# Attention 2 of a two-layer model: context columns rotated on VectorE beside the query projections, and a schedule by half batches

## The chip, the cores and the metric

The kernel runs on one core of a Trainium2 chip. The metric is the device time of one execution in microseconds (us); the time before is the median of six runs. Engines are named as the profile names them: PE is TensorE (PEld its weight loads), DVE is VectorE, ACT is ScalarE, POOL is GpSimd, and SP is SyncE, whose queue issues most transfers.

## The reference, cut to what matters

Four blocks follow one another on x (8 batches of 100 tokens, 512 wide): attention 0, a mixture-of-experts block, attention 2, and a block with quantised weights. The change is in attention 2, which reads a context of 8 batches of 361 rows, 128 wide:

```python
def _L1_xattn_ref(hidden_q, kv_c, Wq, w_kc_q, w_kc_kv, W_qr, W_kr, Wo):
    q_hk = (hidden_q @ Wq.T).reshape(b, s, H, K)
    q_big = jnp.einsum('bshk,hkq->bshq', q_hk, w_kc_q)
    kv_rope = kv_c * cos[None] + _rotate_half(kv_c) * sin[None]
    q_r = jnp.einsum('bshq,hqr->bhsr', q_big, W_qr)
    k_r = jnp.einsum('bld,hdr->bhlr', kv_rope, W_kr)
    scores = jnp.einsum('bhsr,bhlr->bhsl', q_r, k_r)
    attn = jax.nn.softmax(scores, axis=-1)
    ctx_c = jnp.einsum('bhsl,bld->bhsd', attn, kv_rope)
    ctx_lat = jnp.einsum('bhsd,hkd->bshk', ctx_c, w_kc_kv)
    return ctx_lat.reshape(b, s, H * K) @ Wo.T
```

## The kernel before

Weights that follow one another are folded earlier in the kernel: `wqf` takes a normalised token to its query of every head, `wvo` takes the weighted context of all heads to the output. All of attention 2 is in float32. It has three stages.

**Query projections (loop around L1435).** The 800 tokens are seven row tiles, in three groups: tiles 0 and 1, tiles 2 and 3, tiles 4 to 6. For each group PE multiplies `wqf` with the transposed, normalised tokens, in chunks of 8 matmul records: four chunks of two head pairs each (`p0` = 0, 2, 4, 6) for the first two groups, eight chunks of one head pair (`p0` = 0 to 7) and 288 columns for the third. A chunk goes to one PSUM bank, and `evacuate` copies it out, on DVE and ACT in turn (L90, L92). While a group is projected, DVE and ACT normalise the tiles of the next one (`token_norms`: statistics L118 and L120, root L122 on ACT, reciprocal L129, scaling L132), and after chunk `p0 == 4` PE transposes them (`token_rows`, L1301).

**Rotation of the context, beside it.** For each batch SP loads 361 rows in three pieces (`context_in`, L1347; three buffers, so the load of batch b+3 waits until POOL is through with batch b). POOL rotates the rows with four `tensor_tensor` instructions (L1355, L1356, and L1358 twice) and stores them to DRAM, `ctx_rot` (L1359, L1360). From there SP loads them again in three forms: rows (`context_rows`, L1374, L1375), blocks of 32 rows for the values (`context_blocks`, L1384, L1389), and, from the rows, columns: `context_columns` has PE transpose three pieces (L1396), and ACT and DVE copy them out of PSUM to `kvT` (L1398, L1399).

**Scores and values.** `queries(b, h)` multiplies with W_kr for half of the heads of two batches at once (L1489, 16 records into the four banks of `four`), and DVE and ACT copy the result into the tile `qe` (L1495, L1499): for batch 0 in turn, for later batches on ACT alone. A batch has 12 score steps of 96 whole tokens (16 heads in 2 halves of 6 steps), and every even batch one more for the four leftover tokens of two batches. One score step is two PE records (L1524; L1519 for leftovers), a negated row maximum on DVE (L1529), the exponential with its sum on ACT (L1532), a reciprocal on DVE (L1538), the scaling of the probabilities on POOL (L1542; on ACT, L1540, for the first four), and a transpose by 32x32 squares on DVE (L1549). After a half batch's six steps `values(b, h)` multiplies them with the context: 96 records (L1558), copied out by ACT (L1564). Leftovers are transposed by PE (L1573), copied by ACT (L1576, L1577) and multiplied (L1585).

The order on PE, DVE and ACT is written out by hand (`manual_schedule`): step n issues scores(n), scaled(n-1) and turned_squares(n-3), and `due` puts everything else to a step. `values` come AHEAD = 7 steps behind the last score of their half. Also beside these steps, DVE quantises nine weight tiles of the next block (`quantise_steps`, L1598 to L1603), a third of its work per step. The order on SP and POOL is set by the scheduler from the order in the program and from what is free. Each engine carries out its own instructions in order. `tc.issue_after(d)` makes a load follow another on its queue.

## Time and profile before

| | us |
|---|---|
| Median of six runs | 633.34 |
| The six runs | 632.38, 638.66, 633.10, 642.20, 632.33, 633.58 |
| The profiled execution, its own time | 631.59 |
| Its span in the profile | 629.8 |
| Projections of the first group begin (L1435) | 274.5 |
| of the second group | 289.1 |
| of the third group | 304.45 |
| Projections end | 320.2 |
| First values begin (L1558) | 335.94 |
| Last records of attention 2 on PE end | 492.97 |
| From there to the end of the span | 136.8 |

All times inside the execution are from the start of its span. A table of windows lists, for a stretch of time, how long each engine was busy in it, the clock granted to PE (1.00 is full) and the share of the transfer engines' time. The chain of waits goes back from the last instruction to what released it, and so on; it is shown in order of time. A timeline lists one engine's instructions: start, duration, line and operation, out<-in with the shapes; in square brackets stands the idle time just before, with what ended it. An "x6" at the end of a line is a number of instructions put together.

### The profile page before, as it was taken

Reading aid. Unit: us, or ns where it says so; the run is one execution under the profiler, and the core shown is the slowest. Engines: PE = TensorE matmul, PEld = TensorE weight load, DVE = VectorE, ACT = ScalarE, POOL = GpSimd, SP = SyncE. Lnnn points to the kernel's source line nnn. Section 1 sums busy time; section 2 is a strip of 40 time slices with the busy share of each in tenths; the row PEclk is TensorE's granted clock in tenths of the full one; section 3 lists DMA queues with packets and bytes.
Section 4 is the critical chain, followed back from the end, with each engine's and each line's share of the span. In section 5 each row is a group of like instructions: output and inputs, shape, how many; then the busy total and the mean of one; then the engine's idle time right before and its main releaser. Section 6 shows DMA issues by size and latency. Waiting matters only on the chain.

```text
span 629.8 us, 12203 instructions
## 1 busy us (share of the span) xinstructions
PE 603.2 (96%) x4587; PEld 399.2 (63%) x4594; DVE 400.4 (64%) x1032; ACT 234.2 (37%) x545; POOL 241.6 (38%) x246
## 2 busy tenths in 40 slices
PE   8999999979999999999989999999989999999995
PEld 6767755557777776578856767776766644444442
DVE  4865688827777553254147676776776366766687
ACT  3653545651111111331246555556554121222130
POOL 1231331031333321118937676777786002222020
PEclk9999999999999999999999999999999999999999
DMA  8900094758999999663610322323111301101221
GB/s 291 317 26 18 7 324 146 232 167 227 341 303 272 232 294 332 133 197 90 161 34 2 99 73 40 85 74 97 51 37 28 136 11 31 24 17 24 52 38 69
DMA packets 90628, 80.79 MB, mean 128 GB/s; under 512 B 40939, under 2 KB 67263, under 8 KB 90439
## 3 DMA queue, kind: packets, MB, share of 16 engines
q1 hardware_dynamic: 86471, 70.61, 39.1%
q0 software_dynamic: 4096, 9.38, 7.2%
q8 instruction: 37, 0.61, 0.4%
q14 instruction: 24, 0.20, 0.1%
HBM read 62.27 MB, written 10.88 MB: 116 GB/s over the span
## 4 chain that ended last, share of the span: by engine, by line
PE 65%; DVE 8%; ACT 3%; issue 2%; POOL 1%; ACTq 0%; DVEq 0%
PE bank L389 13%; PE bank L1190 12%; PE four L1558 10%; PE bank L1435 7%; PE bank L1251 7%; PE bank L1524 6%; PE bank L1743 3%; PE bank L1291 2%; DVE sq L1549 2%; DVE nm L1529 2%; PE four L1489 1%; PE bank L1127 1%; ACT e L1532 1%; POOL hid L1760 1%; PE bank L395 1%
## 5 line engine op out<-in xcount | busy, mean ns | idle before, releaser
L1542 POOL TENSOR_SCALAR e<-e,rs 128x361 f32<-128x361 f32 x96 | 115.5, 1217 | 46.9 <-DVE rs L1538 45.1
L389 PE MATMUL bank<-wvo,ctxT 128*128 128x512 f32 x192 | 84.4, 594 | 0.0
L1529 DVE TENSOR_REDUCE nm<-bank 128x1 f32<-128x361 f32 x100 | 51.1, 512 | 36.9 <-PE bank L1524 29.1
L1524 PE MATMUL bank<-kvT,qe 128*128 128x361 f32 x192 | 70.2, 489 | 4.5 <-DVE qe L1495 2.5
L1190 PE MATMUL bank<-xgT,w 128*128 128x240 f32 (+1 forms) x384 | 74.1, 369 | 0.4 <-ACT xgT L1131 0.4
L1532 ACT ACTIVATE e<-bank,nm 128x361 f32<-128x361 f32 x100 | 56.7, 568 | 44.2 <-DVE rs L1538 44.2
L1190 PEld LDWEIGHTS bank<-xgT,w 128*128 128x128 f32 (+1 forms) x384 | 64.7, 181 | 11.5 <-issue 6.2
L1558 PEld LDWEIGHTS four<-sq,kv 32*128 32x128 f32 (+1 forms) x1536 | 62.3, 185 | 8.8 <-issue 4.9
L1558 PE MATMUL four<-sq,kv 32*128 32x192 f32 (+1 forms) x1536 | 66.9, 325 | 0.2
L389 PEld LDWEIGHTS bank<-wvo,ctxT 128*128 128x128 f32 x192 | 36.0, 190 | 42.6 <-issue 41.9
L1760 POOL TENSOR_TENSOR hid<-g,u 128x512 f32<-128x512 f32 (+1 forms) x17 | 20.4, 1216 | 110.1 <-ACT g L1751 108.6
L1549 DVE STREAM_TRANSPOSE sq<-e 128x384 f32<-128x384 f32 x96 | 53.5, 557 | 1.3 <-POOL e L1542 1.2
L1263 POOL DMA_INDIRECT x_acc<-y,place x16 | 25.1, 1571 | 75.3 <-ACT y L1262 45.2
L354 POOL TENSOR_TENSOR s<-s,rs 100x800 f32<-100x800 f32 x16 | 24.4, 1523 | 69.2 <-DVE rs L353 35.5
L1524 PEld LDWEIGHTS bank<-kvT,qe 128*128 128x128 f32 x192 | 32.4, 189 | 28.7 <-ACT e L1532 11.2
L1251 PE MATMUL bank<-w,hT 128*128 128x512 f32 (+3 forms) x96 | 42.8, 594 | 0.0
L1435 PE MATMUL bank<-xT,wqf 128*128 128x256 f32 (+1 forms) x128 | 29.8, 393 | 0.0
L1251 PEld LDWEIGHTS bank<-w,hT 128*128 128x128 f32 (+3 forms) x96 | 16.9, 183 | 20.0 <-issue 15.4
L1743 PE MATMUL bank<-w1q,xqT 128*128 128x512 bf16 (+1 forms) x140 | 29.1, 361 | 0.4 <-DMA xqT<-xq 0.2
L1435 PEld LDWEIGHTS bank<-xT,wqf 128*128 128x128 f32 x128 | 24.2, 190 | 4.9
L1748 DVE SCALAR_TENSOR_TENSOR g<-bank,sx,swb 128x512 f32<-128x512 f32 (+1 forms) x18 | 12.6, 702 | 19.0 <-PE bank L1743 18.4
L1201 ACT ACTIVATE silu<-bank 128x240 f32<-128x240 f32 x16 | 5.9, 370 | 50.1 <-PE bank L1190 46.7
(297 smaller groups left out, 965.2 us busy)
## 6 DMA issues: line engine op xcount, KB each, us to landing
w<-in_w SPq DMA_DIRECT2D x8, 1408.0 KB
gu<-in_wgu SPq DMA_DIRECT2D x22, 256.0 KB
wq_p<-in_wq SPq DMA_DIRECT2D x8, 512.0 KB
w<-in_w SPq DMA_DIRECT2D x16, 256.0 KB
wo<-in_wo SPq DMA_DIRECT2D x8, 512.0 KB
kq_p<-in_wkcq SPq DMA_DIRECT2D x16, 192.0 KB
kv<-ctx_rot SPq DMA_DIRECT2D x32, 96.0 KB
dn<-in_wdn SPq DMA_DIRECT2D x4, 704.0 KB
```

The costliest lines, as they stand in the source:

```text
L389: nc.tensor.matmul(po[:, :D], lhs[:, c, ds(t * P, r)], rhs[:, c, :], start=(c == 0), stop=(c == chunks - 1),)
L1190: nc.tensor.matmul(po, w12_e[:, c, cols], xgT[:, c, :], start=(c == c0), stop=(c == c1 - 1))
L1251: nc.tensor.matmul(py[i][:n], hT[:mr, m, ds(s0, n)], w3_e[:mr, m, :], start=(m == blocks[0]), stop=(m == blocks[2]),)
L1435: nc.tensor.matmul(pq[:, i, :], wqf[:, c, ts(p0 + i, P)], xT[:, c, :], start=(c == 0), stop=(c == KC - 1),)
L1524: nc.tensor.matmul(ps[:, :L], of_batch(b)[0][:, a, h, s].rearrange("p g q -> p (g q)"), kvTs[b], start=True, stop=True,)
L1529: nc.vector.tensor_reduce(nm, ps[:, :L], AX.X, ALU.max, negate=True)
L1532: nc.scalar.activation(e[:, :L], ps[:, :L], AF.Exp, bias=nm, accum_out=sm)
L1542: nc.gpsimd.tensor_scalar_mul(e[:, :L], e[:, :L], rs)
L1549: nc.vector.transpose(squares[b, h][:, a * (HT // 2) + s, :], e)
L1558: nc.tensor.matmul(pc[:, g, :cols].rearrange("p (t q) -> p t q", q=32), kv4s[b, j // NBH][ds(32 * g, n), j % NBH, :], eT[ds(32 * g, n), :, ...
L1743: nc.tensor.matmul(pw[:r, :n], xqT[:, c, :r], w1q[:, c, ds(off, n)], start=(c == 0), stop=(c == KC - 1),)
L1760: nc.gpsimd.tensor_tensor(hid[:r, ds(c0, n)], g[:r, :n], u[:r, :n], ALU.mult)
```

## The change

The reference's columns, rotated, are needed for the scores as `kvT` (128 x 361 a batch). The change takes them from a new path and orders the stage anew.

- **Columns.** For each batch SP loads the context as columns twice (`columns_in`: `same`, and `across` with its two halves exchanged; two buffers each), from the transposed input that attention 0 reads already. DVE multiplies both with tables of cosines and signed sines, adds them (`columns_turned`: three `tensor_tensor` of 128x361) and SP stores the result to DRAM, `ctx_rot_t`. `context_columns(b)` is now one load from there; the transposes on PE and the copies on ACT and DVE are gone. The rows are still rotated by POOL (`rotate(b)`), with the same instructions.
- **Where it is done.** `rotate` and `columns_turned` are called between the chunks of the first two groups of projections: behind p0 = 2, 4, 6 of the first (batches 0 to 2), behind p0 = 0, 2, 4 of the second (3 to 5) and twice behind its p0 = 6 (6, 7). In DVE's order they so stand among the copies of the chunks and the norms, and all of them ahead of the third group's copies. The tile `qe` of batches 0 and 1 comes from a pool, `first_pair`, that opens where the column tiles were.
- **Third group.** The PSUM banks of the scores are opened at its start; queries(0, 0) and queries(0, 1) follow its chunks p0 = 1 and 2, the scores 0 to 3 its chunks p0 = 4 to 7.
- **Half batches.** For half batch k there are six score steps, then the values of half batch k-1. Each half has at most one or two other jobs at fixed steps (`beside`): loads, queries (copied by DVE and ACT in turn, for all batches), the leftovers. The five DVE instructions of one quantised tile come in one piece behind the third step of nine halves. Leftover scores follow the values of odd halves of even batches. queries(2, 0) and queries(2, 1) move ahead of the first values.
- **Buffers.** `kv4` moves to a pool that opens after the projections, the quantised tile `gu_q` has one buffer instead of two, and the leftovers get a fifth tile of exponentials.

The diff, cut:

```diff
+    ctx_rot_t = tc.dram_tile([B, DC, L], F32, name="ctx_rot_t")
...
+    early, close_early = open_pool("attn1_early")
+    EP = 32 * ((L + 31) // 32)
+    es = [early.tile([P, EP], F32, tag=f"e{i}", name=f"e{i}") for i in range(4)]
...
+    contexts_in = [None]
+
     def context_in(b):
         kv = rot.tile([LP, LC, DC], F32, tag="kv", name=f"kv{b}")
         for c in range(LC):
-            nc.sync.dma_start(kv[:, c, :], ctx_n[b, ds(c * (LP - 1), LP), :])
+            d = nc.sync.dma_start(kv[:, c, :], ctx_n[b, ds(c * (LP - 1), LP), :])
+        contexts_in[0] = d.ins
         return kv
 
-    contexts = [context_in(b) for b in range(3)]
-    for b in range(B):
-        kv = contexts.pop(0)
+    def rotate(b, kv):
         kvr = rot.tile([LP, LC, DC], F32, tag="turned", name=f"turned{b}", bufs=2)
         low, high = slice(0, DC // 2), slice(DC // 2, DC)
         nc.gpsimd.tensor_tensor(kvr, kv, cos_sb, ALU.mult)
...
         nc.gpsimd.dma_start(
             ctx_rot[b, LP:].rearrange("(c p) d -> p c d", c=LC - 1), kvr[1:, 1:, :]
         )
-        if b + 3 < B:
-            contexts.append(context_in(b + 3))
+
+    contexts = [context_in(b) for b in range(3)]
...
-        kv4 = kvp.tile([P, NBH, DC], F32, tag="kv4", name=f"kv4_{b}_{h}", bufs=3)
+        kv4 = a1w.tile([P, NBH, DC], F32, tag="kv4", name=f"kv4_{b}_{h}", bufs=3)
...
-    def context_columns(b, kvr):
-        pt = bank()[:, : LC * LP].rearrange("p (c l) -> p c l", c=LC)
-        for c, (_, n) in enumerate(LCH):
-            nc.tensor.transpose(pt[:, c, :n], kvr[:n, c, :], ident[:n, :n])
+    colp, close_colp = open_pool("columns_in")
+    cos_col = colp.tile([P, L], F32, tag="cos_col", name="cos_col")
+    sin_col = colp.tile([P, L], F32, tag="sin_col", name="sin_col")
+    with tc.issue_after(contexts_in[0]):
+        nc.sync.dma_start(cos_col, rope_cos_t)
+        nc.sync.dma_start(sin_col, rope_sin_t)
+    columns_load = [None]
+
+    def columns_in(b):
+        same = colp.tile([P, L], F32, tag="same", name=f"same{b}", bufs=2)
+        nc.sync.dma_start(same, ctx_t[:, b, :])
+        across = colp.tile([P, L], F32, tag="across", name=f"across{b}", bufs=2)
+        nc.sync.dma_start(across[: DC // 2], ctx_t[DC // 2 :, b, :])
+        d = nc.sync.dma_start(across[DC // 2 :], ctx_t[: DC // 2, b, :])
+        columns_load[0] = d.ins
+        return b, same, across
+
+    def columns_turned(b, same, across):
+        nc.vector.tensor_tensor(across, across, sin_col, ALU.mult)
+        nc.vector.tensor_tensor(same, same, cos_col, ALU.mult)
+        nc.vector.tensor_tensor(same, same, across, ALU.add)
+        nc.sync.dma_start(ctx_rot_t[b], same)
+
+    def context_columns(b):
         kvT = kvp.tile([P, L], F32, tag="kvT", name=f"kvT{b}")
-        nc.scalar.copy(kvT[:, :LP], pt[:, 0, :])
-        nc.vector.tensor_copy(
-            kvT[:, LP:].rearrange("p (c l) -> p c l", c=LC - 1), pt[:, 1:, : LP - 1]
-        )
+        nc.sync.dma_start(kvT, ctx_rot_t[b])
...
-            qe = a1w.tile([P, 2 * NH1 * S], F32, tag="qe", name=f"qe{b}")
+            pool = a1w if b % 4 else first_pair
+            qe = pool.tile([P, 2 * NH1 * S], F32, tag="qe", name=f"qe{b}", bufs=1)
...
-        if n < 4:
+        if n < EARLY:
...
-        q = a1w.tile([P, D], BF16, tag="gu_q", name=f"gu_q{n}", bufs=2)
+        q = a1w.tile([P, D], BF16, tag="gu_q", name=f"gu_q{n}", bufs=1)
...
+    def next_columns(b):
+        kvTs[b] = context_columns(b)
+
+    def next_rows(b):
+        for k in range(2):
+            kvrs[b + k] = context_rows(b + k)
...
+    EARLY = 4
+
+    with tc.issue_after(contexts_in[0]):
+        columns = [columns_in(b) for b in range(2)]
+    xT_next = xT_first
+    for g, tiles in enumerate(GROUPS):
+        xT = xT_next
+        n = sum(ROWS[t] for t in tiles)
+        per = 512 // n
+        more = g + 1 < len(GROUPS)
+        if more:
+            token_norms(GROUPS[g + 1])
+        else:
+            nc.scalar.activation(most, ln_eps, AF.Exp)
+            assert not columns
+            close_colp()
+            first_pair, close_first_pair = open_pool("first_pair")
+            close_psum()
+            psum, close_psum = open_banks("psum_scores", 4)
+            bank_pools[:] = [psum]
+            four, close_four = open_banks("psum_four", 1)
+            for e in es:
+                nc.vector.memset(e[:, L:], 0.0)
+        for p0 in range(0, NH1 // 2, per):
+            pq = bank()[:, : per * n].rearrange("p (i q) -> p i q", i=per)
+            for i in range(per):
+                for c in range(KC):
+                    nc.tensor.matmul(
+                        pq[:, i, :], wqf[:, c, ts(p0 + i, P)], xT[:, c, :],
+                        start=(c == 0), stop=(c == KC - 1),
+                    )
+            if p0 == 4 and more:
+                xT_next = token_rows(GROUPS[g + 1])
+            evacuate(qr[:, ds(p0, per), ds(tiles[0] * P, n)], pq)
+            if more:
+                last_chunk = g and p0 + per == NH1 // 2
+                for _ in range(len(columns) if last_chunk else int(g > 0 or p0 > 0)):
+                    b = columns[0][0]
+                    rotate(b, contexts.pop(0))
+                    columns_turned(*columns.pop(0))
+                    if b + 3 < B:
+                        with tc.issue_after(columns_load[0]):
+                            contexts.append(context_in(b + 3))
+                    if b + 2 < B:
+                        with tc.issue_after(contexts_in[0]):
+                            columns.append(columns_in(b + 2))
+            else:
+                if p0 in (1, 2):
+                    queries(0, p0 - 1, copies)
+                elif p0 >= NH1 // 2 - EARLY:
+                    n0 = p0 - (NH1 // 2 - EARLY)
+                    scores(n0)
+                    if n0:
+                        scaled(n0 - 1)
+        if g == 0:
+            behind_rows = tc.issue_after(rows_in.ins)
+            behind_rows.__enter__()
+            wkr_sb = qw.tile([P, NH1 // 2, DC], F32, tag="wkr", name="wkr_sb")
+            nc.sync.dma_start(wkr_sb, wkr)
+            behind_rows.__exit__(None, None, None)
+            next_columns(0)
...
+    halves = [(b, h) for b in range(B) for h in range(2)]
+    quantised_in = [k for k in range(2, len(halves)) if k % 4 != 1][:LATER]
+    beside = {}
+
+    def at_step(k, i, f, *args):
+        beside.setdefault((k, i), []).append(lambda: f(*args))
+
     for b in range(B):
-        n0 = first_of[b]
-        for h in range(2):
-            at_step(n0 + HT * (h + 1) - 1 + AHEAD, values, b, h)
-        at_step(n0 + 1, context_blocks, b, 0)
-        at_step(n0 + 7, context_blocks, b, 1)
+        k = 2 * b
+        at_step(k, 1, context_blocks, b, 0)
+        at_step(k + 1, 0, context_blocks, b, 1)
         if b + 1 < B:
-            at_step(n0 + (8 if b % 2 else 1), next_context, b + 1)
-            at_step(n0 + (10 if b % 2 else 9), next_columns, b + 1)
+            at_step(k + 1, 0, next_columns, b + 1)
         if b % 2 == 0:
-            n = n0 + 2 * HT
-            at_step(n + 4, rest_columns, n)
-            at_step(n + 8, rest_values, n)
-        elif b + 1 < B:
-            at_step(n0 + 1, queries, b + 1, 0, on_scalar)
-            at_step(n0 + 9, queries, b + 1, 1, on_scalar)
-    quantising = []
-
-    in_order = tc.manual_schedule(
-        engines={mybir.EngineType.PE, mybir.EngineType.DVE, mybir.EngineType.Activation}
-    )
-    in_order.__enter__()
-    queries(0, 0, copies)
-    po_first = None
-    for n in range(len(work) + AHEAD):
-        if n == len(work) + AHEAD - 1:
-            po_first = bank()
-            project_part(0, po_first, ctxT, wvo, NH1, 0, 4)
-        for f in due.pop(n, ()):
-            f()
-        if n < len(work):
+            at_step(k + 1, 0, next_rows, b)
+            q = (k - 2, k) if b > 2 else (0, 1)
+            if b:
+                for h in range(2):
+                    at_step(q[h], 2 if b > 2 else 5, queries, b, h, copies)
+        else:
+            n = first_of[b] - 1
+            at_step(k + 1, 2, rest_columns, n)
+            at_step(k + 1, 4, rest_values, n)
+
+    turning = []
+
+    def turn_next():
+        turned_squares(turning.pop(0))
...
+    for k, (b, h) in enumerate(halves):
+        n0 = first_of[b] + HT * h
+        behind_rest = h == 0 and b % 2 == 1
+        for i in range(HT):
+            n = n0 + i
+            for f in beside.pop((k, i), ()):
+                f()
+            if n >= EARLY:
+                scores(n)
+                if i == 2 and k and not behind_rest:
+                    turn_next()
+                scaled(n - 1)
+            if k == 0:
+                if i >= EARLY - 1:
+                    turn_next()
+            elif i != 2:
+                turn_next()
+            turning.append(n)
+            if i == 2 and k in quantised_in:
+                for _ in quantise_steps(*late_loads.pop(0)):
+                    pass
+        if k:
+            values(*halves[k - 1])
+        if h and b % 2 == 0:
+            n = n0 + HT
             scores(n)
-        if 0 <= n - 1 < len(work):
             scaled(n - 1)
-        if 0 <= n - LATE < len(work) and work[n - LATE][1] is not None:
-            turned_squares(n - LATE)
-        if n >= 12 and n % 10 == 2 and late_loads:
-            quantising.append(quantise_steps(*late_loads.pop(0)))
-        if quantising and next(quantising[0], True):
-            quantising.pop(0)
-    assert not due and not quantising and not late_loads and not state
+            turn_next()
+    scaled(n)
+    while turning:
+        turn_next()
+    po_first = bank()
+    project_part(0, po_first, ctxT, wvo, NH1, 0, 4)
+    values(*halves[-1])
     project_part(0, po_first, ctxT, wvo, NH1, 4, 6)
+    assert not beside and not late_loads and not state
```

## The prediction

> **What bounds the kernel now.** I read the page's busy shares first, then windows around the stage, the chain of waits inside it, and the timelines of VectorE (DVE), GpSimd (POOL) and the SyncE queue (SP).
>
> ```profile
> span 629.8 us, 12203 instructions
> PE 603.2 (96%) x4587; PEld 399.2 (63%) x4594; DVE 400.4 (64%) x1032; ACT 234.2 (37%) x545; POOL 241.6 (38%) x246
> ```
>
> TensorE (PE) is busy 96%, so a gain is PE work taken away or PE idle time closed. Windows (stretch, us, then busy time of PE, PEld, DVE, ACT, POOL, the granted clock, DMA) show where it idles:
>
> ```profile
> 304.45:319.80 15.35, 15.35 (x66) 12.02 (x65) 1.83 (x4) 3.27 (x6) 13.93 (x20) 1.00 0.60 157
> 319.80:335.90 16.10, 12.66 (x68) 7.54 (x66) 10.84 (x30) 10.08 (x33) 4.73 (x9) 1.00 0.04 12
> 335.90:493.00 157.10, 151.37 (x1908) 110.70 (x1907) 108.72 (x324) 85.17 (x256) 111.32 (x93) 1.00 0.23 59
> 622.00:629.80 7.80, 1.50 (x14) 1.09 (x12) 4.60 (x9) 0.00 (x0) 0.00 (x0) 0.82 0.37 134
> ```
>
> In the third group of projections PE is full and DVE nearly empty (1.83 of 15.35 us). Between it and the first values DVE is full and PE loses 3.4 us. The steady stage to 493 loses little; the same work by hand (below) needs 149.0 us of its 157.0, so about 8 us idle. The chain of waits (start, us, what) gives the prices:
>
> ```profile
> 301.03 19.18 PE bank L1435 x80
> ...
> 321.31 1.65 PE four L1489 x16
> ...
> 323.04 0.57 DVE qe L1495
> ...
> 335.94 4.11 PE four L1558 x96
> ```
>
> PE runs projections unbroken from 301.03 to 320.2; queries wait for two copies in turn (323.04 to 325.43, 2.4 us for one `queries`); the first values start at 335.94 (V00).
>
> **The change, part by part, against the profiled execution (its own time 631.59, span 629.8).**
>
> *Taken away.* Eight times three transposes, on the chain as 0.31 us a batch: six in the stage, 1.9 us. Their ACT copy (0.28) and DVE copy (0.41) go with them; these lay beside PE but for batch 0 (320.24 to 321.31: 1.1 us). The queries of batches 2 and 3 move ahead of V00: 2 x 1.55 = 3.1 us change sides.
>
> *V00 if the columns keep up.* The third group starts at 304.45 and each of its chunks takes 1.94 us. `queries(0,1)` follows chunk p0=2: PE is there at 311.8, and the copies of `queries(0,0)` (PE until 309.9, plus 2.4) end at 312.3. Behind it lie three `queries` (4.65), five chunks (9.7), twelve scores (12 x 0.668 = 8.0) and about 1 us of bank waits: 23.4 us. V00 = 312.4 + 23.4 = 335.8, beside 335.94 now, with batches 2 and 3's queries already done.
>
> *V00 to the stage's end.* Before: values 16 x 4.11 = 65.8, scores 84 x 0.668 = 56.1, leftover scores 4 x 0.78, queries 6 x 1.55, kvT 1.9, leftover transposes 4 x 0.56, leftover values 4 x 1.28, project 5.5: 149.0, and 8.0 idle. After: 149.0 - 3.1 - 1.9 = 144.0. What is late next: each half batch now has six scores in a row, DVE about 0.96 us a score (0.51 maximum, 0.15 reciprocal, 0.56 transpose) against 8.1 of PE a half, so DVE fits (5.8) except where a quantise burst (1.95) and queries' copies (1.1 to 1.7) join it. I estimate idle 0.1 for eight plain halves, 0.25 for four behind leftovers, 0.3 for four with queries, and 0.75 for four where the leftover values wait for ACT's copies of the turned leftovers: 6 us, with 3 and 12 as bounds (the burst halves worth nothing, or DVE binding in all nine). So 150.5 us from V00 instead of 157.0.
>
> *The columns.* This is the unknown. DVE gets 24 multiplications and additions of 128x361, all eight batches ahead of the third group's first copy in DVE's order. Two rows bear on one such instruction: VectorE alone, 0.56, and VectorE beside POOL, stretched.
>
> ```profile
> 290.49 1.07 DVE L132 TENSOR_SCALAR xn<-x,mv,rstd 128x512 f32<-128x512 f32 x1
> ...
> 293.07 0.84 DVE L132 TENSOR_SCALAR xn<-x,mv,rstd 128x512 f32<-128x512 f32 x1
> ...
> 306.66 0.46 DVE L90 COPY ctxT<-bank 128x288 f32<-128x288 f32 x1 [6.13 <-PE bank L1435]
> ...
> 509.60 0.56 DVE L1812 TENSOR_TENSOR g<-g,u 128x384 f32<-128x384 f32 x1
> ```
>
> The normalising L132 takes 0.55 at 275.77 with POOL idle, and 1.07 and 0.84 while POOL rotates:
>
> ```profile
> 290.27 1.00 POOL L1355 TENSOR_TENSOR turned<-kv,cos_sb 121x384 f32<-121x384 f32 x1
> 291.35 1.07 POOL L1356 TENSOR_TENSOR kv<-kv,sin_sb 121x384 f32<-121x384 f32 x1
> 292.50 1.13 POOL L1358 TENSOR_TENSOR turned<-turned,kv 121x192 f32<-121x192 f32 x2
> ```
>
> So one batch costs DVE 3 x 0.5 = 1.5 us alone, and about 3 x 1.0 = 3.0 if each waits out a POOL instruction; POOL rotates without a pause from 280 to 320. I take about 2 for most of them.
>
> The Trainium skill, "SBUF — State Buffer", section "Who interferes with whom", speaks against the change: a VectorE instruction with two SBUF inputs shares a port pair with GpSimd's reads, and whichever issues first blocks the other outright. By that rule alone every batch takes 3 us or more and POOL is delayed as well, which is the slower rival below.
>
> *The loads behind them.* Column tiles have two buffers, so the load of batch b+2 waits on SP until the store of batch b has landed, and everything behind it on SP waits too: the rows of kv, the other stores, kvr. And kv's loads wait for POOL:
>
> ```profile
> 298.68 1.10 SPq L1347 DMA_DIRECT2D kv<-in_ctx_n  x3
> ...
> 303.62 1.10 SPq L1347 DMA_DIRECT2D kv<-in_ctx_n  x3
> ```
>
> The last (batch 7) cannot go before POOL's batch 4 is through, 303.6; column batch 5 is queued behind it. A load of 256 KB issued at 267.01 was used at 269.61, a store of 60 to 120 KB lands 2.2 to 2.9 us after its issue; I take 2.4. Followed through: loads 0 and 1 land at 284.5; batch 0 turned 286, 1 by 288.5, store landed and batch 2 loaded 291.5, turned 293; the norms of tiles 4 to 6 (6 us as before) end 299, just as PE wants them (299.8, the transposes). Batches 3 and 4 are turned 301 to 304.5; batch 5 is issued 304.1 to 305.6, lands 306.2 to 307.8, turned by 307.4 to 309.3; batch 6 by 309.5 to 312; batch 7, whose load waits for batch 5's store, lands 312.2 to 313.9 and is turned by 313.2 (alone) to 315.1 (held).
>
> DVE's copies of the third group stand behind it, and the copies of `queries(0,0)` also wait until batches 6 and 7 are stored, since their tile lies where the columns lay: +2.4, 315.6 to 317.5; the copies +2.4, 318.1 to 320. PE, with three chunks and one `queries` in hand, is ready for `queries(0,1)` at 311.8 and stands until 319: a stall of about 7 us (5.8 to 9).
>
> *The clock.* PE's idle may cost more than itself. The kernel's first matmuls are slow, and the last window is granted 0.82 although PE ended near 623.5.
>
> ```profile
> 1.51 4.21 PE L465 MATMUL bank<-zeros 128*128 128x384 f32 x6 [1.51 <-POOL zeros L178]
> ```
>
> These 384-column records take 0.87 us each; a 361-column one later takes 0.489. In the last window 0.18 x 7.8 = 1.4 us of clock are lost, at half clock 2.8 us, so the clock fell some 3.5 us after the last matmul. A stall of 7 us passes that; the first 4.2 us after it at half clock cost 2.1 us (0 if it stays under). "TensorE: Matmul & The Clock Gate", section "What's actually happening", states an idle window of about 3.4 us and as long to return; by its figure the loss is 1.7 and the sum 0.4 less.
>
> *Other edits, at nothing.* The early scores' scaling on ACT (0.62) is as now. kv4 in a pool that opens after the projections waits for PE's last chunk, then needs about four issues of 0.35 and 2.2 to land, 3.6 us; until V00 PE has 9.1 us of scores and queries. If that cover went, V00 would wait. One fewer quantise buffer hides behind bursts two halves apart.
>
> *Sum.* V00 = 319 + 23.4 + 2.1 = 344.5; end 344.5 + 150.5 = 495.0 against 492.97: +2.0. The 136.8 us behind it are untouched. 631.59 + 2.0 = 633.6; the profiled execution lies 1.75 under the median of the six runs and 1.1 under that of the four lowest, so 634.5. Copies done at 318.1, no clock loss and 3 us idle give 628; at 320, the loss and 8 us idle, 637.
>
> **The rivals.**
> - *The columns are on time* (batch 7 turned by 306.4, stores landed 309): the end is 335.8 + 150.5 = 486.3, -6.7, 626. For: DVE has 9.6 of 14.6 us free in the first group. Against: SP's wait for POOL at 303.6 alone forbids it, unless POOL starts earlier.
> - *Slower: DVE and POOL take strict turns.* Each turned instruction waits for one of POOL's and holds POOL back as long; batch 7 is turned at about 320.7, stores landed 323.1, copies 325.5, V00 at 351, end 502: +9, 641.6. For: the stretched L132. Against: L132 waited about once per batch and POOL's own rows grew only from 1.00 to 1.07. It decides once the rotations of batches 3 to 7 cost over 2 us each more than alone.
> - *DVE becomes the bound in the halves with a burst*: 5.8 + 1.95 + 1.7 = 9.5 against PE 8.1 + 1.55 = 9.7; a little more on DVE and each of nine halves loses 0.6: +5.5, 640. For: before spread a tile's quantise instructions over three steps. Against: PE's ready banks let it run some scores ahead.
>
> **How the numbers follow.** Stall pays back the gain 0.58 (its own range 628 to 637), columns on time 0.15, strict turns 0.15, DVE bound 0.12. A measurement tells about 1%, 6.3 us, from no change: faster is under 627.0, slower over 639.7. Faster: 0.11 of the first rival and 0.02 of the likeliest, 0.13. Slower: 0.12 of strict turns, 0.07 of DVE bound, 0.04 of the likeliest, 0.23. Same 0.64. Leaving out the outer half of the first rival (0.07) and of strict turns (0.08), the range is 626 to 642.
>
> **What the profile after would show.** PE idle of 6 to 9 us between chunk p0=2 of the third group and `queries(0,1)`, near 311 to 319, with DVE behind the column load's wait; a granted clock under 1.00 after it; DVE's rotations 0.5 to 1.1 each; V00 near 344 and the stage's end 150.5 later. No PE stall there, or V00 near 336, makes me wrong to the fast side; a stage of over 155 us from V00 makes the steady halves wrong.

## The result, and the profile after

The changed kernel takes 651.03 us (median of 20 runs, 649.02 to 659.55) against 633.34 (46 runs): ratio 1.0287, 95% interval 1.0263 to 1.0311. The forecast was 634.5 in a range to 642. The profiled execution has a span of 648.5 us against 629.8. Some executions of any kernel are disturbed and some ten us longer: the medians include them, every ratio leaves them out, and the profiles of *ahead* and *ahead_queries*, used further down, are of such executions.

The page's first lines of the changed kernel:

```profile
span 648.5 us, 12228 instructions
...
PE 607.2 (94%) x4563; PEld 402.4 (62%) x4570; DVE 426.1 (66%) x1064; ACT 229.2 (35%) x525; POOL 241.7 (37%) x242
```

PE does about the same work (607.2 us busy, 603.2 before) in 18.7 us more. Where it stood idle or ran slowly shows in windows cut at its own events: the third group's transposes, the stall before `queries(0,1)`, the first values (358.74), and the rest of the stage.

```profile
273.00:306.80 33.80, 29.40 (x144) 24.56 (x142) 21.49 (x37) 7.26 (x16) 23.43 (x30) 0.97 0.66 196
306.80:329.43 22.63, 13.71 (x58) 10.46 (x57) 14.17 (x24) 3.87 (x9) 15.77 (x19) 0.80 0.57 163
329.43:358.74 29.31, 25.83 (x113) 17.94 (x113) 14.57 (x40) 13.61 (x42) 7.07 (x7) 0.89 0.14 40
358.74:365.30 6.56, 6.56 (x101) 5.78 (x101) 0.28 (x1) 1.07 (x3) 1.17 (x1) 0.74 0.02 4
365.30:511.30 146.00, 140.32 (x1759) 102.24 (x1757) 109.71 (x317) 75.31 (x224) 104.49 (x89) 1.00 0.27 71
```

The first three windows hold the loss: idle of 4.4, 8.9 and 3.5 us, and a granted clock of 0.97, 0.80 and 0.89 where before it was 1.00 in all windows shown. The first values, in the fourth, run at 0.74 and take 1.7 us more. The last window is the new order at full clock, with 5.7 us idle in 146. PE's timeline names each stall in its brackets (`four` is the tile of four PSUM banks that queries and values share):

```profile
301.79 0.63 PE L1302 MATMUL bank<-ident,xn 128*128 128x128 f32 x4 [1.22 <-DVE xn L133]
303.90 0.66 PE L1302 MATMUL bank<-ident,xn 128*128 128x128 f32 x4 [1.49 <-DVE xn L133]
306.24 0.63 PE L1302 MATMUL bank<-ident,xn 32*128 32x32 f32 x4 [1.69 <-DVE xn L133]
306.80 10.01 PE L1621 MATMUL bank<-xT,wqf 128*128 128x256 f32 x32
...
329.43 3.04 PE L1466 MATMUL four<-ctxT,wkr_sb 64*128 64x200 f32 x16 [8.92 <-ACT qe L1476]
332.40 5.72 PE L1621 MATMUL bank<-xT,wqf 128*128 128x288 f32 x16
...
358.74 5.86 PE L1535 MATMUL four<-sq,kv 32*128 32x192 f32 x96 [2.94 <-ACT qe L1476]
```

Behind each stall the records are longer: 32 projection records (the second group's last chunk has 16, the third group's chunks have 8 each) in 10.01 us (7.60 in the kernels below that run there at full clock), queries in 3.04 instead of 1.62, two chunks in 5.72 instead of 4.15, values in 5.86 instead of 4.18. DVE's timeline shows what it did instead of the norms and the copies:

```profile
285.84 1.68 DVE L1416 TENSOR_TENSOR across<-across,sin_col 128x361 f32<-128x361 f32 x1 [6.14 <-DMA across<-in_ctx_t]
...
291.12 1.99 DVE L1418 TENSOR_TENSOR same<-same,across 128x361 f32<-128x361 f32 x1
...
297.11 1.30 DVE L1417 TENSOR_TENSOR same<-same,cos_col 128x361 f32<-128x361 f32 x1 [2.75 <-DMA same<-in_ctx_t]
...
317.00 0.54 DVE L1417 TENSOR_TENSOR same<-same,cos_col 128x361 f32<-128x361 f32 x1 [2.44 <-DMA same<-in_ctx_t]
...
324.23 0.54 DVE L1418 TENSOR_TENSOR same<-same,across 128x361 f32<-128x361 f32 x1
```

Two things at once: an instruction of 0.5 us takes up to 1.99, and DVE waits for loads, 8.5 us in all behind batch 0. Of the 24 instructions, 16 overlap in time with POOL's rotation and take 1.14 us on the mean; the eight that fall into its pauses take 0.51 to 0.54. The last batch is turned at 324.77. The chain of waits through those loads:

```profile
313.34 3.56 DMA same<-in_ctx_t
...
318.13 2.95 DMA ctx_rot_t<-same
...
321.14 2.49 DMA same<-in_ctx_t
...
324.79 2.12 DMA ctx_rot_t<-same
```

A store must land (2.95) before the load into its buffer can go (2.49), then DVE's last instructions, then another store (2.12), and only then the copies of queries(0,0).

To set kernels beside each other I count from the first projection record, T0 (274.50 before, 275.27 after): what lies ahead of T0 is the same code in every kernel and T0 differed by up to 6 us between profiles (ten and more in *ahead* and *ahead_queries*). The stage runs from the first values to PE's first record behind attention 2.

| kernel | batch 7 turned | first values | stage from there | ratio, 95% interval |
|---|---|---|---|---|
| before | (on PE) | T0 + 61.4 | 156.9 | 1 |
| the change | T0 + 49.5 | T0 + 83.5 | 152.5 | 1.0287 (1.0263 to 1.0311) |
| after_queries | 49.9 | 80.5 | 150.8 | 1.0210 (1.0143 to 1.0277) |
| psum_operands | 49.4 | 81.4 | 153.8 | 1.0221 (1.0180 to 1.0262) |
| psum_late | 44.7 | 76.8 | 152.1 | 1.0186 (1.0131 to 1.0241) |
| four_buffers | 42.5 | 76.4 | 152.4 | 1.0165 (1.0135 to 1.0194) |
| both | 40.1 | 72.3 | 150.7 | 1.0150 (1.0122 to 1.0179) |
| columns_first | 36.8 | 70.3 | 153.8 | 1.0110 (1.0088 to 1.0131) |
| ahead | 33.4 | 70.8 | 153.6 | 1.0077 (1.0054 to 1.0099) |
| ahead_queries | 33.1 | 67.8 | 150.7 | 0.9997 (0.9966 to 1.0029) |
| ahead_queries_sbuf | 42.9 | 73.9 | 150.7 | 1.0099 (1.0080 to 1.0118) |
| ahead_act | 34.0 | 67.2 | 150.7 | 1.0003 (0.9968 to 1.0038) |
| ahead_late | 38.3 | 68.3 | 151.0 | 1.0004 (0.9985 to 1.0023) |
| pe_columns | (on PE) | 65.4 | 160.2 | 1.0141 (1.0070 to 1.0212) |
| pe_columns_2 | (on PE) | 62.9 | 161.1 | 1.0126 (1.0070 to 1.0182) |

So the 18.7 us are: T0 0.8 later, first values 22.1 later behind T0, stage 4.4 shorter, the rest 0.3 longer. Most intervals of neighbouring rows overlap, so small differences between ratios are read from the profiles. The 22.1 add up from PE's timeline: idle before the transposes 4.40, the slow 32 projections 2.41, the stall 8.92, the slow queries and chunks behind it 1.42 + 1.57, and 0.42 + 2.94 before the first values: 22.08. By this subtraction the first values would come at T0 + 61.4 without them; no run shows it directly.

### The profile page after: what moved, and what is told of

Read it like the earlier page. It is cut to its first block, busy times and chain, and to the rows that moved or that the text cites. A ratio compares the mean times of both kernels' runs of the same rounds, so it can differ in the third digit from the quotient of the medians.

```text
span 648.5 us, 12228 instructions
## 1 busy us (share of the span) xinstructions
PE 607.2 (94%) x4563; PEld 402.4 (62%) x4570; DVE 426.1 (66%) x1064; ACT 229.2 (35%) x525; POOL 241.7 (37%) x242
## 4 chain that ended last, share of the span: by engine, by line
PE 56%; DVE 10%; DMA 5%; ACT 3%; issue 2%; POOL 1%; SPq 1%; DVEq 0%; ACTq 0%
PE bank L1191 11%; PE bank L390 11%; PE four L1535 10%; PE bank L1252 6%; PE bank L1501 6%; PE bank L1806 3%; PE bank L1292 2%; PE bank L1621 2%; PE four L1466 2%; DMA same<-in_ctx_t 1%; DVE sq L1526 1%; DMA swb<-scale_row 1%; PE bank L1128 1%; DVE same L1417 1%; DVE nm L1506 1%
## 5 line engine op out<-in xcount | busy, mean ns | idle before, releaser
L1519 POOL TENSOR_SCALAR e<-e,rs 128x361 f32<-128x361 f32 x96 | 112.7, 1192 | 64.5 <-DVE rs L1515 34.5
L1535 PE MATMUL four<-sq,kv 32*128 32x192 f32 (+1 forms) x1536 | 68.6, 331 | 6.6 <-ACT ctxT L1567 3.1
L1535 PEld LDWEIGHTS four<-sq,kv 32*128 32x128 f32 (+1 forms) x1536 | 64.0, 189 | 15.3 <-ACT ctxT L1567 4.9
L1501 PE MATMUL bank<-kvT,qe 128*128 128x361 f32 x192 | 67.6, 484 | 0.7 <-ACT e L1509 0.4
L1264 POOL DMA_INDIRECT x_acc<-y,place x16 | 25.1, 1570 | 74.9 <-ACT y L1263 44.9
L355 POOL TENSOR_TENSOR s<-s,rs 100x800 f32<-100x800 f32 x16 | 24.4, 1522 | 70.1 <-DVE rs L354 35.5
L1621 PE MATMUL bank<-xT,wqf 128*128 128x256 f32 (+1 forms) x128 | 34.8, 432 | 0.0
L1621 PEld LDWEIGHTS bank<-xT,wqf 128*128 128x128 f32 x128 | 26.8, 212 | 7.1 <-issue 0.7
L1811 DVE SCALAR_TENSOR_TENSOR g<-bank,sx,swb 128x512 f32<-128x512 f32 (+1 forms) x18 | 12.6, 702 | 19.3 <-PE bank L1806 18.7
L1203 DVE TENSOR_TENSOR hT<-silu,bank 128x240 f32<-128x240 f32 x16 | 6.5, 404 | 27.5 <-ACT silu L1202 21.3
```

The lines of the kernel that those rows point to most:

```text
L1264: d = nc.gpsimd.indirect_dma_start(out=x_acc, out_offset=bass.IndirectOffsetOnAxis(ap=place[:, 0:1], axis=0), in_=y, in_offset=None, compu ...
L1501: nc.tensor.matmul(ps[:, :L], of_batch(b)[0][:, a, h, s].rearrange("p g q -> p (g q)"), kvTs[b], start=True, stop=True,)
L1519: nc.gpsimd.tensor_scalar_mul(e[:, :L], e[:, :L], rs)
L1535: nc.tensor.matmul(pc[:, g, :cols].rearrange("p (t q) -> p t q", q=32), kv4s[b, j // NBH][ds(32 * g, n), j % NBH, :], eT[ds(32 * g, n), :, ...
L1621: nc.tensor.matmul(pq[:, i, :], wqf[:, c, ts(p0 + i, P)], xT[:, c, :], start=(c == 0), stop=(c == KC - 1),)
```

## The experiments

**First theory (the port):** POOL's rotation stretches DVE's instructions. **Rival (the round trip):** two buffers and SP's fixed order make each load wait for a store. **Third:** the new order costs by itself. Four kernels.

*four_buffers* (cut; behind each turned batch b, the columns of batch b + 4 are asked for instead of b + 2)

```diff
-        same = colp.tile(..., bufs=2)
+        same = colp.tile(..., bufs=4)      # across likewise
-        columns = [columns_in(b) for b in range(2)]
+        columns = [columns_in(b) for b in range(4)]
```

> Four buffers of column tiles instead of two, four batches loaded ahead: no load waits for a store until batch 4. Round-trip theory (the load of batch b+2 waits for the store of batch b): DVE no longer waits for loads; batch 2 is turned at about 296 instead of 299.7, batch 7 at about 317 instead of 324.8, the stall before queries(0,1) shrinks from 8.9 to 2 us; ratio about 1.01 instead of 1.029. Port theory (the turned instructions are stretched by POOL, 22.5 us in all where 12.3 would do): the loads are not what is late, the instructions stretch as before and the ratio stays over 1.02.

*psum_operands*

```diff
-        nc.vector.tensor_tensor(across, across, sin_col, ALU.mult)
-        nc.vector.tensor_tensor(same, same, cos_col, ALU.mult)
-        nc.vector.tensor_tensor(same, same, across, ALU.add)
+        nc.vector.tensor_tensor(crossed, across, sin_bank, ALU.mult)   # crossed, tables: PSUM
+        nc.vector.tensor_tensor(same, same, cos_bank, ALU.mult)
+        nc.vector.tensor_tensor(same, same, crossed, ALU.add)
```

> The tables and the product with sine lie in PSUM, so each turned instruction reads one operand from SBUF; two buffers as in the change (projections have four PSUM banks instead of eight). Port theory: the 24 instructions take 0.45 to 0.6 each beside POOL, 12 to 14 us in all instead of 22.5, POOL's are back at 1.00, 1.00 and 0.57, batch 2 is turned near 294, batch 7 near 316 instead of 324.8; ratio about 1.01. Round-trip theory: the loads still come when the stores have landed, batch 7 is turned after 320; ratio over 1.02.

*both* (four buffers and PSUM operands)

> Four buffers and PSUM operands together. If the two causes are all there is: batch 2 turned near 291.5, the norms done by 298.5 without a stall, batch 7 turned near 307 and stored by 310, no stall over 1.5 us before queries(0,1), granted clock 1.00 throughout, first values near 338, stage 150.8 behind them; ratio 0.99 to 0.997. If a third cause is left (SP's order behind POOL's rows, the wait for the stores in the memory of the columns), a stall of over 3 us stays and the ratio is over 1.00.

*pe_columns*: `columns_in` and `columns_turned` left out, `context_columns` and a third buffer of rows as before needs them; to make room, the turned leftovers share the tile of their exponentials.

> The new order alone: columns by PE transposes and copies as before, nothing rotated on DVE, no ctx_rot_t. If the columns' path is the whole loss (both theories of the path), PE no longer stands before the third group's transposes nor before queries(0,1); the first values start near 338 us and the stage takes 150.8 + 8 x 0.31 of transposes = about 153 us behind them, so some 491 at its end against 493 before: a ratio to the kernel before of 0.995 to 1.000. Theory 3, that the early scores and the half batches themselves cost: the first values later than 345 or the stage over 157, ratio over 1.01.

Measured. The two causes are both there, and removing either alone takes back less than half. The groups of the 24 instructions (total us, then mean ns, then the idle time before them), in the change and, with the port taken away, in psum_late (described below):

```profile
L1417 DVE TENSOR_TENSOR same<-same,cos_col 128x361 f32<-128x361 f32 x8 | 8.3, 1034 | 6.1 <-DMA same<-in_ctx_t 6.1
...
L1418 DVE TENSOR_TENSOR same<-same,across 128x361 f32<-128x361 f32 x8 | 7.6, 954 | 0.3
L1416 DVE TENSOR_TENSOR across<-across,sin_col 128x361 f32<-128x361 f32 x8 | 6.6, 820 | 8.5 <-DMA across<-in_ctx_t 8.5
```

```profile
L1426 DVE TENSOR_TENSOR crossed<-across,sin_bank 128x361 f32<-128x361 f32 x8 | 4.3, 536 | 9.1 <-DMA across<-in_ctx_t 9.1
L1428 DVE TENSOR_TENSOR same<-same,crossed 128x361 f32<-128x361 f32 x8 | 4.3, 532 | 0.3
L1427 DVE TENSOR_TENSOR same<-same,cos_bank 128x361 f32<-128x361 f32 x8 | 4.2, 527 | 9.9 <-DMA same<-in_ctx_t 9.9
```

With one operand in PSUM the instructions fall from 22.5 us to 12.8, and the waits for loads rise from 14.6 to 19.0: much of what DVE no longer spends at the port it waits for loads. The opposite holds in four_buffers: no wait for a load behind batch 0, but 23.3 us of instructions. POOL's own rows show the other half of the port: its second multiplication takes 1164 ns on the mean in the change and 1039 in psum_late, its additions 695 and 588. In psum_operands ACT's copies of the tables stood ahead of the second group's norms, and PE stood 1.72 us for them, so its ratio is not the port's alone; psum_late is the clean run. In *both*, which has the same copies in ACT's way, PE stood 1.18 and 1.78 us for the second group's norms, a stall of 2.71 us before queries(0,0) stays, and batch 7 is turned only at T0 + 40.1, with 4.56 us of idle time on DVE before it. The expectation's third cause, SP's order behind POOL's rows, would fit the number, but the chain of waits names the round trip again:

```profile
310.12 5.71 DMA ctx_rot_t<-same
...
316.25 2.84 DMA across<-in_ctx_t
```

With four buffers batch 7's load waits for batch 3's store, and that store took 5.71 us to land.

pe_columns missed its expectation, in the place of the third theory. There was no stall before the transposes (T0 + 25.13, as before) and 0.31 us before queries(0,1), so the early scores work; but it lost 2.69 us before the first values and a half clock behind, and the stage was 160.2. PE's work in that stage took 152.9 us at a granted clock of 0.97, against 148.1 at full clock in pe_columns_2 below, so the clock fell there more than once. PE's waits in it, from the first values on:

```profile
PE four L1545 <- ACT e L1536: 4.5, 4, 1.3
PE four L1518 <- ACT qe L1459: 2.7, 1, 2.7
PE bank L1484 <- ACT e L1492: 2.1, 5, 0.8
```

The first row (4.5 us, four times) I put down to my shared tile: ACT cannot copy the turned leftovers before all of the tile is transposed. The same wait is 1.4 us in the change, so about 3 are the tile's. The second is the change's own: the copies of queries(2,1), which also cost it 2.94.

**Then SP's order, and what is turned when.**

*columns_first*: both, with the table copies behind the norms and this, so two edits at once:

```diff
+                    if b + 4 < B:
+                        columns.append(columns_in(b + 4))
                     if b + 3 < B:
                         contexts.append(context_in(b + 3))
-                    if b + 4 < B:
-                        columns.append(columns_in(b + 4))
```

> As both, but on SP the columns of batch b+4 are asked for before the rows of batch b+3, and ACT copies the tables into PSUM behind the norms of the second group's tokens. Times from the start of the first projection (T0; it was 274.5 us before, and differed by up to 6 us between kernels). Theory that SP's order behind POOL's rows is the third cause: batch 7 is turned near T0 + 35.5 instead of T0 + 40.1 (both), the copies of queries(0,0) end near T0 + 41, a stall of about 3.5 us before queries(0,1), first values near T0 + 67, ratio 1.000 to 1.006. If SP's order does not matter, batch 7 is still turned at T0 + 40 and the ratio stays at 1.012 or more.

*ahead*: columns_first, and four batches turned in the first group, four in the second.

```diff
-                for _ in range(2 if last_chunk else int(g > 0 or p0 > 0)):
+                for _ in range(2 if not g and p0 + per == NH1 // 2 else int(g > 0 or p0 > 0)):
```

> As columns_first, but four batches are turned ahead of the norms of the third group's tokens and four behind them. The norms still end by T0 + 25, and batch 7 is turned near T0 + 32 and stored by T0 + 35: no stall over 1 us before queries(0,1); first values near T0 + 64.5, of which 2.9 us are the wait for the copies of queries(2,1); ratio 0.995 to 1.000. If the wait for the stores in the columns' memory rules, a stall of 2 to 4 us stays, and the ratio is over 1.002.

*ahead_queries*: ahead, and this edit; *after_queries* is the change with this edit alone.

```diff
-                    at_step(q[h], 2 if b > 2 else 5, queries, b, h, copies)
+                    at_step(q[h], 2 if b > 2 or h else 5, queries, b, h, copies)
```

> As ahead, with queries(2,1) after two scores of the second half batch instead of five. Theory that the wait before the first values is its copies behind turned squares that wait for POOL: the wait of 2.7 to 2.9 us and the half clock after it are gone, first values near T0 + 61.5 to 62.5, the stage 150 to 151 behind them; ratio 0.988 to 0.995, a version that beats both. If the wait is POOL's scaling itself, it moves to another instruction and the first values stay past T0 + 63.5.

> The change with one edit: queries(2,1) after two scores of the second half batch instead of five. The wait of 2.9 us before the first values and the half clock after it (1.7 us) are gone if these are that edit's; the columns' path is as in the change. Ratio 1.020 to 1.023 instead of 1.029, first values 2 to 3 us earlier behind queries(0,1). If the wait moves to another instruction, 1.027 or more.

*ahead_queries_sbuf*: ahead_queries with both operands in SBUF.

> As ahead_queries, but the turned instructions read both operands from SBUF as in the change. Port theory: 22 us for the 24 instructions again, batch 3 turned at T0 + 24 instead of T0 + 18.5, the norms end near T0 + 30 and PE stands 4 to 5 us before the third group's transposes, batch 7 turned near T0 + 43; first values past T0 + 72, ratio 1.012 to 1.02. If it was only the order of the loads, as ahead_queries, within 0.3%.

*psum_late*: the change with PSUM operands, table copies behind the norms, two buffers.

> The change with the port alone taken away: one operand in PSUM as in psum_operands, with ACT's copies of the tables behind the norms (in psum_operands they stood ahead of them and cost 1.7 us). Two buffers and SP's order as in the change. Port theory: batch 7 turned at T0 + 42 or earlier (T0 + 49.5 in the change), ratio under 1.017. Round-trip theory: DVE waits for loads instead, batch 7 turned at T0 + 47 or later, ratio 1.02 to 1.028.

Measured. In columns_first batch 7 is turned at T0 + 36.8 instead of 40.1 (35.5 expected), but this is not shown to be SP's order: batch 6 is already earlier by as much (T0 + 30.4 instead of 34.0), since PE no longer stands for the second group's norms, and DVE's waits for batch 7's load are no shorter (3.52 + 1.30 us, 4.56 in *both*), again behind a store, which took 6.24 us to land. The table copies, moved between psum_operands and psum_late too, were worth about as much there (1.0221 and 1.0186, against 1.0150 and 1.0110 here). No run moves SP's order alone. Turning four batches early brought it to 33.4 without delaying the norms (ended by T0 + 25.1), but a stall of 2.73 us before queries(0,1) stayed, with 2.55 us for the load of W_kr; the first values came at T0 + 70.8, not 64.5. The earlier queries(2,1) did what was expected of it: the wait before the first values fell from 2.93 to 0.77 us and the values ran at full clock (4.18 us). In the change alone it brought the first values 3.0 us forward behind T0 and the stage from 152.5 to 150.8; the ratios, 1.0287 and 1.0210, have intervals that touch. ahead_queries is level with the kernel before, at 0.9997, and not the expected 0.988 to 0.995. The port is worth 1% there: with both operands in SBUF the 24 instructions take 24.5 us, the norms end at T0 + 30.6 and the ratio is 1.0099 (1.012 to 1.02 was expected). psum_late fell between the two theories' numbers: batch 7 at T0 + 44.7, five us earlier than in the change, with 13.7 us of waiting for loads behind batch 0.

**What is left of the front: order or transfers?**

*ahead_act*: ahead_queries with all stores of turned columns issued by ACT, and W_kr asked for ahead of the columns.

```diff
-        nc.sync.dma_start(ctx_rot_t[b], same)
+        nc.scalar.dma_start(ctx_rot_t[b], same)
```

> As ahead_queries, with the stores of the turned columns issued by ACT instead of SP, and the load of W_kr asked for early. In ahead_queries batch 7 was turned at T0 + 33.0, but its store went out at T0 + 35.5 behind POOL's rows on SP, and PE stood 1.5 us for W_kr and 3.2 us for the copies of queries(0,0). Theory that SP's order is what is left: both stalls under 1 us, no half clock, first values near T0 + 62.5 instead of T0 + 67.8, stage 150.7; ratio 0.990 to 0.994, faster than both kernels. Rival, that the transfers themselves are late beside the others: stalls of 3 us stay, ratio 0.998 to 1.002.

*ahead_late*: as ahead_act, but the stores of batches 0 to 3 on SP, and those of 4 to 7 on ACT behind the copies of the transposed tokens.

> As ahead_queries, with W_kr asked for early, the first four stores on SP, and the last four issued by ACT only behind the copies of the transposed tokens (in ahead_act ACT's copies stood behind stores that waited for DVE, and PE 3.2 us for them, with a half clock behind). Theory that the order of stores and loads on in-order queues is all that is left: no stall over 1 us between the third group's transposes and queries(0,1), no half clock there, first values T0 + 62 to 64 (T0 + 67.2 in ahead_act), stage 150.7; ratio 0.990 to 0.996, faster than both kernels. Rival, that the transfers are late whatever their order, since eight at most are under way on a queue and each takes 2.5 to 5 us here: first values T0 + 66 or later, ratio 0.998 to 1.002.

*pe_columns_2*: pe_columns with the edit of ahead_queries, two buffers of rows, a tile of their own for the turned leftovers, and these steps:

```diff
-            at_step(k + 1, 2, rest_columns, n)
-            at_step(k + 1, 4, rest_values, n)
+            at_step(k, 2, rest_columns, n)
+            at_step(k, 4, rest_values, n)
-            q = (k - 2, k) if b > 2 else (0, 1)
+            q = (k - 1, k) if b > 2 else (0, 1)
```

> As pe_columns (columns by PE and copies, nothing rotated on DVE), with queries(2,1) after two scores of the second half batch, the leftovers in a tile of their own and in the halves before, and queries of batches 4 and 6 half a batch later. Theory that pe_columns lost by the wait before the first values (2.7 us and a half clock of 1.7), by the leftovers' tile (4.5 us) and by 2.2 us of transposes: first values near T0 + 62, the stage near 153 behind them; ratio 0.993 to 0.998. If the half-batch order itself loses, the stage is over 157 and the ratio over 1.002.

Measured. ahead_act moved the wait: ACT's copies stood behind stores that wait for DVE, and PE stood 3.2 us in three places. ahead_late moved it once more and did not take it away: PE stood 1.89 us for ACT's copies and 2.10 us behind batch 7, because ACT's next copy waited behind ACT's own stores:

```profile
307.77 0.58 ACT L92 COPY ctxT<-bank 128x512 f32<-128x512 f32 x1 [6.36 <-DMA ctx_rot_t<-same]
```

Its chain of waits:

```profile
299.29 2.89 DMA ctx_rot_t<-same
...
303.45 4.63 DMA across<-in_ctx_t
...
308.10 4.07 DMA kv<-in_ctx_n
```

One load of 92 KB takes 4.63 us from issue to landing, and a piece of the rows behind it 4.07, where the prediction had taken 2.4. Batch 7 is turned at T0 + 38.3, later than in ahead_queries. Windows of the kernel before and of ahead_late, over the first two groups:

```profile
273.00:306.00 33.00, 33.00 (x165) 28.43 (x164) 12.25 (x25) 8.34 (x18) 23.40 (x31) 1.00 0.38 113
```

```profile
273.00:306.00 33.00, 33.00 (x164) 28.38 (x162) 21.00 (x46) 7.83 (x18) 21.09 (x28) 1.00 0.77 221
```

The transfer engines are busy 0.77 instead of 0.38, at 221 GB/s instead of 113: the columns come twice, are stored, and come again. The numbers are those of the last run's rival, that the transfers are late whatever their order, but the run does not settle it, since ACT's copies still stood behind stores. What is shown: three orders of the same transfers all ended level with the kernel before (0.9997, 1.0003, 1.0004), and in each the stage's 6 us are spent at the front. No version beat the kernel before.

pe_columns_2 brought the first values to T0 + 62.9, but its leftovers are turned a half batch earlier, close behind their scaling, and PE waited 7.0 us in four places for POOL there: stage 161.1. That is the number the expectation gave for a half-batch order that loses by itself; the waits show the leftovers' place instead. Whether the new order with PE's transposes could beat the kernel before is open; neither of my two arrangements of the leftovers shows it.

## Why the prediction was wrong

*Right: what the new order is worth.* From the first values to the stage's end I had 150.5 us instead of 157.0. Measured: 152.5 in the change, of which 1.7 are the first values at low clock; 150.7 to 151.0 in the six kernels with turned columns where they ran at full clock. That the number fits is in part luck. The forecast took 2 us of idle time and 5.0 of work away (and its 144.0 and 6.0 make 150.0, not 150.5). Measured, the idle time hardly changed, 5.7 us before and 5.6 in ahead_queries, and the work fell by 6.1, from 151.2 to 145.1: the 149.0 of the forecast had left out 2 us of work and called them idle. The first values without stalls come, by subtraction, at T0 + 61.4, as worked out (335.8). The rival of DVE as the bound in the halves with a burst did not come.

*Right in kind: the stall before queries(0,1), in its place and with its cause,* DVE's copies behind the last batch's load and store. 5.8 to 9 us were forecast, 8.92 measured. But PE reached it late already, so that this number hides the miss: the copies ended at 329.4, not at 318.1 to 320.

*Wrong, the step "The columns" (mis-sized):* "I take about 2 for most of them" a batch; measured 22.5 us for eight, 2.8 a batch, against 12.8 with a PSUM operand. The row of L132 (0.84 to 1.18 instead of 0.55) had shown it, and the Trainium skill, "SBUF — State Buffer", section "Who interferes with whom", says that a two-input instruction and GpSimd's reads exclude each other on the shared ports. The runs agree with that in both directions: 0.53 us with one SBUF input, up to 1.99 with two, and POOL's additions 0.70 instead of 0.59. The prediction's "POOL rotates without a pause" is not so: POOL pauses to issue its stores, and eight of the 24 instructions fell there.

*Wrong, the step "The loads behind them":* I followed the loads with 2.4 us each way and the rotations with 1.5 to 2. The table shows how this step by step departs:

| us from the span's start | forecast | measured |
|---|---|---|
| batch 0 turned | 286 | 289.6 |
| batch 1 | 288.5 | 293.1 |
| batch 2 | 293 | 299.7 |
| norms of tiles 4 to 6 end | 299 | 306.2 |
| batch 5 | 307.4 to 309.3 | 318.1 |
| batch 7 | 313.2 to 315.1 | 324.8 |
| copies of queries(0,0) end | 318.1 to 320 | 329.4 |

The first two batches are late mostly by the port: of batch 0's 3.6 us, 1.3 are its load, which landed at 285.8 instead of 284.5. Batch 2 is late by both: store 1 waited on SP for the stretched batch 1, and the load of batch 2's `same` stood behind that store (294.03, landing 2.98 later). From there DVE's order carries the delay into the norms, and PE stood 4.4 us before the transposes, where I had written "just as PE wants them". A step whose margin was under 1 us should have had its miss in the sum.

*Wrong, the step "The clock" (mis-sized):* one loss of 2.1 us after one stall. It fell in three places, with 2.4, 3.0 and 1.7 us lost on PE.

*Mis-sized, "about 1 us of bank waits" in the step to V00 (the first values):* measured 0.42 + 2.94, the latter for the copies of queries(2,1). They stand in DVE's order behind turned squares that wait for POOL's scaling. The forecast did not ask what is queued ahead of the copies of the early queries.

*The rivals.* The strict turns came nearest (641.6). Its condition, over 2 us more per rotation of batches 3 to 7, was not met: these five took 2.4 us each, 0.8 more than alone (1.2 more over all eight). The time is beyond it because the loads were late as well, which I had priced as if the rotations were on time, and because the clock and the copies of queries(2,1) cost more. The range's upper end was that rival alone; the late loads came on top.

## What to carry to other kernels

Work that is moved onto an engine with idle time is not free if that engine's order also holds the next stage's inputs: ask for each instruction ahead of a critical copy when its own data lands. Before an instruction with two SBUF inputs is set beside GpSimd's work, price it at the stretched row; an operand in PSUM took the stretch away. A tensor that is loaded, turned, stored and loaded again with two buffers runs at the pace of the round trip, so count one store and one load landing per buffer, at the latency measured while the other transfers run (4.63 us for 92 KB here, where 2.4 had been taken), and let delays of different kinds come on top of each other in the range.

## What the hardware showed

The granted clock falls after less idle time than I had inferred from the tail. In the change 2.94 us of idle before the first values were followed by 1.7 us lost, and 4.4 us in three pieces between 300 and 307 by 2.4. In ahead_late, stalls of 1.89 and 2.10 us between 306.5 and 312.7 were enough: the chunk at 314.51 took 3.62 us instead of 2.21. The trace's record of the clock has it at half in stretches of 3.41 us or multiples of that. That agrees with the window of about 3.4 us that the Trainium skill states ("TensorE: Matmul & The Clock Gate", section "What's actually happening"); that a stretch with some PE work in it can lower the clock is what the runs here add.

Where the stall falls decides as well. A stall of 2.9 us before the first values lost nothing in *both*, 1.7 us in the change and 2.9 in columns_first. In the clock records of each execution every fall lies a multiple of 3.413 us behind the first. The stall fell into such an interval with 2.65 us in the change (356.09 to 359.50), and in *both* it was divided, 1.25 and 1.69. Over the traces of all these kernels, from 20 to 620 us, each of the 28 such intervals that began at full clock and had PE idle for 2.0 us or more was followed by the half clock; of the 38 with 1.2 to 1.9 us, five were.
